# A two-layer graph transformer on one core: where lists, ranks, own queries, bias rows and the turned block stand in the order of the work

## The chip, the cores and the metric

The kernel runs on one core of a Trainium2 chip. The metric is the device time of one execution in microseconds (us); the time of a kernel is the median of its runs. A profiled execution gives a span (first to last instruction of the core), a trace of every instruction, and the clock granted to TensorE.

## What is computed

Two layers of the same graph transformer on 2,708 tokens of 512 numbers. The adjacency matrix is sparse (some ten neighbours for a token, itself among them). All numbers are float32.

```python
def layer(h, adj, ...):                      # 8 heads of 64, feed-forward of 2048
    mask = adj + eye(n)
    q, k, v = (h @ Wq.T + bq), (h @ Wk.T + bk), (h @ Wv.T + bv)
    scores = where(mask == 0, -1e9, q k^T / sqrt(64))      # per head
    attn_out = (softmax(scores) @ v) @ Wo.T + bo
    h1 = layer_norm(h + attn_out, ln1_g, ln1_b)
    ff = relu(h1 @ W1.T + b1) @ W2.T + b2
    return layer_norm(h1 + ff, ln2_g, ln2_b)
```

## The kernel before, in words

**Tiles and places.** `by_edges` (L480) does all the work (`by_rows` runs only if a flag says that the lists did not fit; here they do). Tokens are worked in 22 tiles of 128, the last with 20. The kernel finds each token's list of neighbours, ranks the tokens by the length of their lists, and from then on a tile is 128 places in that order, so that all tokens of tile g have at most `CAPS[g]` neighbours. Keys and values of a tile's neighbours are gathered from DRAM row by row (`gather`, L1076, an indirect DMA that GpSimd, POOL, issues), one slot of the list at a time.

**Stage 1, `first` (L874).** For each of the 22 tiles in their first order TensorE makes keys and values (`project`, L577: four matmuls of 128x512, each in two passes). ScalarE copies them out of PSUM, POOL adds bk to the keys, and ScalarE's DMA queue writes them to `kv_d`. Beside that, `lists` (L685) turns rows of the adjacency matrix, loaded by SyncE (SP), into lists on VectorE (DVE); `counted` (L722) counts and numbers them and leaves `hot`, `before` and the record `rec`. bk and bq come as columns (`given_column`, L558) and are turned into rows that all partitions hold (`turned_row`, L563: four 128x128 diagonals on VectorE, four matmuls by ones on TensorE, a copy).

**Stage 2, `first_queries` (L951).** 22 tiles of queries (`evicted`, L957, on VectorE; `written`, L964, stores two tiles at a time by SyncE). At t = 1 `ranked` (L783): four matmul pairs `pr` (L790, L797), a chain of VectorE steps, and the write of `rec` to `rec_d` in the first order of the tokens (L811, L815, on ScalarE's queue). At t = 4 `inverted` (L853) gives `ident_i`, the token at each place; the keys of tile 21 are finished (`last_keys`, L943); the lists of the first two tiles (`list_of`, L1017), the rows of x of the first three (`own_rows`, L1020, `xr`) and the first gathers of keys are issued on POOL. At t = 7 (`OWN`) the three `xr` are turned (`flip`, L1246: four transposes on TensorE, a copy on ScalarE) and two tiles' queries made of them; the third follows at t = 12. `LISTS` holds the t at which two more lists are gathered. `beside_queries` (L1625) loads W1 and W2 and advances the attention.

**Attention, `attend` (L1540).** A generator whose steps are chunks of two slots: VectorE multiplies keys by the query and sums (L1114, L1120); one step later ScalarE takes exponentials and scales values (`p`, L1133; L1140) and VectorE scales and adds the rest; later still the sums are divided (`cx`, L1184). `advance` (L1597) emits steps as credit allows:

```python
        credit = min(credit + more, 1.5)
        while credit > 0 and len(got) < CXB:
            cost = next(ahead, None)
            if cost is None:
                break
            credit -= cost
```

A step costs 1 for two slots. `None` comes back when a tile's query is not to be had: beyond the first three tiles of `order` (20, 19, 18; then 17) queries of layer 0 are fetched from `q_d` (`asked`, L1086), which needs all of them written.

**Feed-forward.** Blocks of two tiles. For each of 16 f: four matmuls `pf` (L1458), a Relu `ft` on ScalarE (L1469) and, LAG = 3 later, the second product `a` (L1431). `pf` has three PSUM buffers. In between stand the next block's output projection and norm (`attended`, L1379, through `cT`) and its transposition (`turned`, L1402: two flips into the one buffer `hT`), the keys and values of layer 1 (`keys_values`, L1498), and steps of attention by the paces `PACES` and `PACE`. `load_next` (L1315) fetches the biases that layer 1 needs.

**Layer 1's queries** are made of transposed tiles `zT_d` by `Layer.query` (L1349) and stored by `kept` (L1362); eight tiles are loaded ahead (`preloaded`, L1322), the others pass through `queries` (L1335) with three buffers.

The order on every engine is the program's order: all five are scheduled by hand, each engine works and waits in order, and so does each engine's DMA queue.

Of the kernel before, what the change touches and what calls it, by code (L numbers as in the profile page):

```python
# [18 lines left out]
P = 128  # L19
DM = 512  # L20
# [26 lines left out]
OWN = 7  # L47
LISTS = (6, 9, 11, 14, 15, 17, 18, 19, 20, 21)
# [431 lines left out]
def by_edges(ctx: ExitStack, tc: tile.TileContext, x, xT, adj, layers, out, redo):  # L480
# [34 lines left out]
    own = {}  # L515
    all_made = []
# [12 lines left out]
    ident_i = const.tile([P, NT], I32, name="ident_i")  # L529
    flags = const.tile([P, 4 + NL], F32, name="flags")  # L530
# [6 lines left out]
    rec_d = dram.tile([N, 2 * LIST], F32, name="rec_d")  # L537
# [20 lines left out]
    def given_column(w, name):  # L558
        t = small.tile([P, NC], F32, tag=name, name=name, bufs=1)
        nc.sync.dma_start(out=t, in_=w[name])  # L560
        return t

    def turned_row(col, name, scale):  # L563

        t = rows.tile([P, DM], F32, tag=name, name=name)
        dg = dn.tile([P, NC, P], F32, tag="row", name="dg", bufs=3)
        for c in range(NC):
            nc.vector.tensor_scalar(
                dg[:, c, :], ident, col[:, c : c + 1], scale, ALU.mult, ALU.mult
            )  # L570
        yield t
        pr = ps.tile([P, DM], F32, tag="g", name="pr")
        for c in range(NC):
            nc.tensor.matmul(pr[:, c * P : (c + 1) * P], ones, dg[:, c, :], start=True, stop=True)
        nc.vector.tensor_copy(t, pr)
# [39 lines left out]
    def lists_of(pa):  # L615
# [167 lines left out]
        def ranked(hot, before, half):  # L783

            at = pa.tile([P, NT], F32, tag="at", name="at", bufs=1)
            for h in range(2):
# [24 lines left out]
            nc.scalar.dma_start(  # L811
                out=rec_d[: (NT - 1) * P, :].rearrange("(g p) c -> p g c", p=P),
                in_=rec[:, : NT - 1, :],
            )
            nc.scalar.dma_start(out=rec_d[(NT - 1) * P :, :], in_=rec[:LW, NT - 1, :])  # L815
# [37 lines left out]
        def inverted(parts):  # L853
# [16 lines left out]
            nc.vector.tensor_tensor(ident_i, sums[:, :NT], sums[:, NT:], ALU.add)  # L870

        return lists, counted, (ranked, inverted)

    def first(w, meanwhile):  # L874
# [27 lines left out]
        for c in range(NC):  # L902
            nc.sync.dma_start(out=wk[:, c, :], in_=chunked(w["Wk"])[:, c, :])
            if c == 0:
                cols = [given_column(w, "bk")]
        cols.append(given_column(w, "bq"))
        finish(halves)
        turning = turned_row(cols[0], "bk", 1.0)
        bk = next(turning)
        turning_q = turned_row(cols[1], "bq", DK**-0.5)  # L910
        bq = next(turning_q)
        wv = matrix(w, "Wv", "wv")
        pa = tc.tile_pool(name="pa", bufs=2)
        lists, counted, placing = lists_of(pa.__enter__())
        done, before = 0, None
        for t in range(NT):
            r = size(t)
            xs = tokens(t, 0)
            kv = wts.tile([P, 2 * DM], F32, tag=f"w2_{5 + t % 3}", name="kvs")
            k = project(xs, r, wk, "k")  # L920
            if t == 0:
                finish(turning)
                finish(turning_q)
# [16 lines left out]
            if t == QT:  # L940
                wq = matrix(w, "Wq", "wq", nc.gpsimd)

# [6 lines left out]
        return bq, wq, counts, placing, pa, tokens, last_keys  # L949

    def first_queries(bq, wq, counts, placing, pa, tokens, last_keys, meanwhile):  # L951

        nonlocal at
        ranked, inverted = placing
# [19 lines left out]
        for t in range(NT):  # L974
# [4 lines left out]
            if t == 1:  # L979
                parts = ranked(*counts)  # L980
                evicted(0, held, qs)
            if t == 4:
# [7 lines left out]
                for g in order[:2]:  # L990
                    list_of(g)
                xrs = [own_rows(g) for g in order[:3]]
# [4 lines left out]
            if t == 0:  # L997
                held = q
            else:
                evicted(t, q, qs)  # L1000
# [4 lines left out]
            if t == OWN:  # L1005
                zTs = [turned_own(g, xr) for g, xr in zip(order, xrs)]
# [3 lines left out]
            if t == OWN + 5:  # L1010
                own_query(order[2], zTs[2], to[order[2]], bq, wq)
# [5 lines left out]
    def list_of(g):  # L1017
        gather(listed[: size(g), g, :], rec_d, ident_i[: size(g), g : g + 1])
# [801 lines left out]
```

## Time and profile before

| what | us |
|---|---|
| median of 3 runs (1875.48 to 1880.53) | 1876.91 |
| the profiled execution | 1872.77 |
| its span | 1871.0 |
| stage 1, to the last values of tile 21 | 0 to 154.7 |
| stage 2, to the last query matmul | 154.6 to 262.5 |
| layer 0's feed-forward begins | 264.6 |
| layer 1's queries begin with tile 3 of its order | 1103.4 |
| layer 1's feed-forward begins | 1179.7 |
| TensorE's last matmul ends | 1861.8 |

The mean granted clock is 0.996. The DMA engines are busy 80 to 100% of the time in the first 180 us (300 to 400 GB/s) and less later (195 GB/s over the span). Rows of a timeline give start, duration, engine, line, operation, tiles written and read, how many instructions are merged, and in brackets the engine's idle time before and what ended it. `PE` is a matmul, `ACT` ScalarE, a name with q a DMA queue.

### The profile page before, as it was taken

The numbers are of one execution on the slowest core, as the hardware profiler recorded it, in microseconds if no ns is written. First come the engines' busy times: TensorE is split into PE (matmuls) and PEld (weight loads), VectorE is DVE, ScalarE is ACT, GpSimd is POOL, SyncE is SP. The second block draws the span as 40 slices with busy tenths as digits, with TensorE's granted clock in tenths as the row PEclk, the third lists the DMA queues.
The fourth block names the chain that finished last, engine by engine and source line by source line (L and its number), as shares of the span: only waits on it lengthen the run. The fifth ranks groups of instructions, "written<-read, shape, count | busy, mean of one in ns | idle before, by whom it ended". The sixth has DMA issues, their size and how long they took to land.

```text
span 1871.0 us, 20950 instructions
## 1 busy us (share of the span) xinstructions
PE 1834.5 (98%) x6172; PEld 1090.1 (58%) x6172; DVE 1378.4 (74%) x2160; ACT 941.9 (50%) x3261; POOL 778.7 (42%) x743
## 2 busy tenths in 40 slices
PE   8999899999999999999999999999999999999997
PEld 4444455665656656566565544566666666566664
DVE  6886569876777868678674147878888988789842
ACT  5670336555445555555643213556655675557531
POOL 3233655443544435343531033444553655356302
PEclk9999899999999999999999999999999999999999
DMA  9999867646545455463541676836554664446300
GB/s 334 356 333 307 308 207 265 205 145 208 186 147 182 165 195 195 159 200 116 182 160 45 210 243 259 308 122 229 186 204 156 241 220 164 179 170 207 126 1 20
DMA packets 134411, 366.93 MB, mean 196 GB/s; under 512 B 19636, under 2 KB 37892, under 8 KB 134286
## 3 DMA queue, kind: packets, MB, share of 16 engines
q0 software_dynamic: 70608, 252.12, 39.5%
q1 hardware_dynamic: 50754, 90.23, 14.0%
q10 hardware_dynamic: 12924, 23.15, 3.3%
q8 instruction: 50, 0.82, 0.2%
q14 instruction: 75, 0.61, 0.1%
HBM read 314.79 MB, written 50.65 MB: 195 GB/s over the span
## 4 chain that ended last, share of the span: by engine, by line
PE 86%; DVE 5%; DMA 4%; ACT 2%; issue 2%; POOL 0%; SPq 0%; ACTq 0%; POOLq 0%; DVEq 0%
PE pf L1458 29%; PE a L1431 28%; PE k L587 8%; PE v L587 8%; PE o L587 7%; PE q L587 3%; PE tp L1250 2%; DVE kv L1114 1%; DMA rec_d<-rec 1%; DVE sc L1120 1%; ACT kv L1140 1%; DVE kv L1146 1%; DMA w<-in_W 1%; PE a L1446 1%; ACT cx L1184 1%
## 5 line engine op out<-in xcount | busy, mean ns | idle before, releaser
L1458 PE MATMUL pf<-hT,w 128*128 128x256 f32 (+1 forms) x2816 | 631.5, 371 | 8.0 <-ACT hT L1255 6.3
L1458 PEld LDWEIGHTS pf<-hT,w 128*128 128x128 f32 x2816 | 517.5, 190 | 180.9 <-issue 101.5
L1077 POOL DMA_INDIRECT kv<-kv_d,listed x420 | 504.3, 1201 | 281.0 <-issue 117.2
L1431 PE MATMUL a<-w,ft 128*128 128x512 f32 x1312 | 611.1, 592 | 0.0
L1469 ACT ACTIVATE ft<-pf,b 128x256 f32<-128x256 f32 (+1 forms) x336 | 154.9, 463 | 453.4 <-PE pf L1458 453.3
L1431 PEld LDWEIGHTS a<-w,ft 128*128 128x128 f32 x1312 | 246.8, 190 | 187.4 <-issue 170.9
L1240 POOL TENSOR_TENSOR rd<-va,mhalf 128x1 f32<-128x1 f32 (+1 forms) x88 | 81.6, 928 | 561.1 <-DVE va L1238 561.1
L1140 ACT ACTIVATE kv<-kv,p 128x64 f32<-128x64 f32 x1232 | 311.0, 334 | 5.0
L1114 DVE TENSOR_TENSOR kv<-kv,q 128x1024 f32<-128x1024 f32 (+1 forms) x222 | 256.7, 1157 | 12.7 <-DMA q<-q_d,ident_i 11.6
L1120 DVE TENSOR_REDUCE sc<-kv 128x16 f32<-128x1024 f32 (+1 forms) x222 | 257.9, 1162 | 7.6
L1153 DVE TENSOR_TENSOR acc<-acc,kv 128x1024 f32<-128x1024 f32 (+2 forms) x178 | 205.3, 1154 | 76.7 <-ACT kv L1140 65.8
L1133 ACT ACTIVATE p<-sc,listed 128x8 f32<-128x8 f32 x420 | 103.6, 295 | 132.5 <-DVE sc L1120 121.8
L1146 DVE TENSOR_TENSOR kv<-kv,p 128x512 f32<-128x512 f32 (+1 forms) x178 | 122.9, 690 | 44.0 <-ACT p L1133 44.0
L587 PE MATMUL o<-wo,cT 128*128 128x512 f32 x336 | 148.1, 593 | 1.0 <-ACT cT L1255 1.0
L587 PEld LDWEIGHTS o<-wo,cT 128*128 128x128 f32 x336 | 63.5, 190 | 81.9 <-issue 75.1
L1244 DVE SCALAR_TENSOR_TENSOR h<-h,rd,ln_b 128x512 f32<-128x512 f32 (+1 forms) x88 | 66.1, 751 | 39.9 <-POOL rd L1240 39.9
L1184 ACT ACTIVATE cx<-acc,su 128x64 f32<-128x64 f32 (+1 forms) x352 | 88.3, 333 | 12.9 <-DVE su L1176 7.7
L707 DVE MAX8 tops<-code 128x8 f32<-128x247 f32 (+2 forms) x242 | 78.6, 400 | 18.2 <-ACT code L702 18.2
L1140 ACT ACTIVATE acc<-kv,p 128x64 f32<-128x64 f32 (+1 forms) x352 | 88.8, 335 | 1.4
L1393 DVE TENSOR_TENSOR h<-o,xb 128x512 f32<-128x512 f32 (+1 forms) x44 | 30.2, 687 | 73.0 <-PE o L587 51.5
L587 PE MATMUL k<-wk,xg 128*128 128x512 f32 x168 | 77.1, 602 | 5.1 <-DMA wk<-in_Wk 5.1
L1518 ACT COPY kvs<-v 128x512 f32<-128x512 f32 (+1 forms) x22 | 12.9, 586 | 132.9 <-PE v L587 131.9
(170 smaller groups left out, 1596.2 us busy)
## 6 DMA issues: line engine op xcount, KB each, us to landing
aj<-in_adj SPq DMA_DIRECT2D x42, 677.0 KB, 6.6
kv_d<-kvs ACTq DMA_DIRECT2D x21, 512.0 KB, 6.9
xg<-in_xT SPq DMA_DIRECT2D x19, 512.0 KB, 6.5
w<-in_W SPq DMA_DIRECT2D x16, 512.0 KB, 5.9
kv<-kv_d,listed POOLq DMA_INDIRECT x420, 5.9
zT_d<-zT SPq DMA_DIRECT2D x22, 256.0 KB, 5.6
xb_d<-h SPq DMA_DIRECT2D x21, 256.0 KB, 5.8
q<-q_d SPq DMA_DIRECT2D x21, 256.0 KB, 4.1
```

The costliest lines, as they stand in the source:

```text
L587: nc.tensor.matmul(o[:r], xs(c), wm[:, c, :], start=(c == 0), stop=(c == NC - 1))
L1077: return nc.gpsimd.indirect_dma_start(out=to, out_offset=None, in_=table[:, :], in_offset=bass.IndirectOffsetOnAxis(ap=s, axis=0), bounds_ ...
L1114: nc.vector.tensor_tensor(kv[:r, :c, :DM], kv[:r, :c, :DM], self.q[:r].unsqueeze(1).to_broadcast([r, c, DM]), ALU.mult,)
L1120: nc.vector.tensor_reduce(self.sc[:r, s0 : s0 + c, :], kv[:r, :c, :DM].rearrange("p s (h d) -> p s h d", d=DK), AX.X, ALU.add,)
L1133: nc.scalar.activation(p[:r, s, :], self.sc[:r, s, :], AF.Exp, bias=minus[:r, g, s : s + 1])
L1140: nc.scalar.activation(to[:, i, hd], kv[:r, i, DM + h * DK : DM + (h + 1) * DK], AF.Copy, scale=p[:r, s0 + i, h : h + 1],)
L1146: nc.vector.tensor_tensor(to[:, 0, :].rearrange("p (h d) -> p h d", d=DK), kv[:r, 0, DM:].rearrange("p (h d) -> p h d", d=DK), p[:r, s0, : ...
L1153: nc.vector.tensor_tensor(self.acc[:r, :c, :], self.acc[:r, :c, :], kv[:r, :c, DM:], ALU.add)
L1184: nc.scalar.activation(cx[:r, hd], self.acc[:r, 0, hd], AF.Copy, scale=self.su[:r, h : h + 1])
L1431: nc.tensor.matmul(a[:r], fts[f][:, c0 : c0 + r], self.w2[f // 2][:, f % 2, :], start=(f == 0), stop=(f == NFC - 1),)
L1458: nc.tensor.matmul(pf[:, :w], self.w1[f // 2][:, c, f % 2 * P : f % 2 * P + P], hT[:, c, :w], start=(c == 0), stop=(c == NC - 1),)
L1469: nc.scalar.activation(ft[:, :w], pf[:, :w], AF.Relu, bias=self.b1[:, f : f + 1])
```

## The change

It has these parts:

- `rec_d` holds one row of 22 records for each lane (partition), and is written by one DMA ahead of the last tile's keys; `place_i` gives the row of a place's record.
- `ranked` stands ahead of the keys of tile 21 (the small tile); `inverted` and what follows stand at t = 2.
- OWN = 5 and earlier `LISTS`; the third tile is turned when its query is made.
- The columns bk and bq are written to a DRAM line by a DMA of single elements and loaded as a row; POOL scales bq. `turned_row` goes.
- W1 and W2 of the first four pairs of f are loaded at t = 8, 10, 12, 14 of stage 2 (before: at the end of stage 1 and t = 0, 1), the fifth at t = 16 (before 6).
- `hT` of the next block is copied ahead of the step of f = 15.
- Layer 1: two more transposed tiles are loaded into the `hT` buffer, queries are stored by SyncE, except for a middle stretch that ScalarE's queue stores.

```diff
-OWN = 7
-LISTS = (6, 9, 11, 14, 15, 17, 18, 19, 20, 21)
+OWN = 5
+LISTS = (4, 7, 9, 12, 13, 14, 15, 17, 18, 19)
...
-    rec_d = dram.tile([N, 2 * LIST], F32, name="rec_d")
+    rec_d = dram.tile([P * NT, 2 * LIST], F32, name="rec_d")
...
+    def lined(w, name, by):
+
+        line = dram.tile([1, DM], F32, name=f"{name}_d{len(lines)}")
+        lines.append(line)
+        by.dma_start(out=line.rearrange("o (c p) -> p (o c)", p=P), in_=w[name])
+        return line
+
+    def row_of(line, name, scale=None):
+
+        t = rows.tile([P, DM], F32, tag=name, name=name)
+        nc.sync.dma_start(out=t, in_=line.to_broadcast([P, DM]))
+        if scale is not None:
+            nc.gpsimd.tensor_scalar(t, t, scale, None, ALU.mult)
         return t
...
-            nc.scalar.dma_start(
-                out=rec_d[: (NT - 1) * P, :].rearrange("(g p) c -> p g c", p=P),
-                in_=rec[:, : NT - 1, :],
-            )
-            nc.scalar.dma_start(out=rec_d[(NT - 1) * P :, :], in_=rec[:LW, NT - 1, :])
+            nc.scalar.dma_start(out=rec_d.rearrange("(p t) c -> p t c", p=P), in_=rec)
...
             nc.vector.tensor_tensor(ident_i, sums[:, :NT], sums[:, NT:], ALU.add)
+            nc.vector.tensor_scalar(sums[:, :NT], sums[:, :NT], NT, None, ALU.mult)
+            nc.vector.tensor_scalar(sums[:, NT:], sums[:, NT:], 1.0 / P, None, ALU.mult)
+            nc.vector.tensor_tensor(place_i, sums[:, :NT], sums[:, NT:], ALU.add)
...
-            if c == 0:
-                cols = [given_column(w, "bk")]
-        cols.append(given_column(w, "bq"))
+        short = [lined(w, name, nc.scalar) for name in ("bk", "bq")]
...
         wv = matrix(w, "Wv", "wv")
+        bk = row_of(short[0], "bk")
...
             r = size(t)
+            if t == NT - 1:
+                parts = placing[0](*counts)
             xs = tokens(t, 0)
...
+            if t == NT - 4:
+                bq = row_of(short[1], "bq", DK**-0.5)
...
-            if t == 1:
-                parts = ranked(*counts)
-                evicted(0, held, qs)
-            if t == 4:
+            if t == 2:
                 inverted(parts)
...
-                for g in order[:2]:
-                    list_of(g)
-                xrs = [own_rows(g) for g in order[:3]]
+                list_of(order[0])
+                xrs = [own_rows(g) for g in order[:2]]
+                list_of(order[1])
+                xrs.append(own_rows(order[2]))
...
-                zTs = [turned_own(g, xr) for g, xr in zip(order, xrs)]
+                zTs = [turned_own(g, xr) for g, xr in zip(blocks[0], xrs)]
...
-                own_query(order[2], zTs[2], to[order[2]], bq, wq)
+                own_query(order[2], turned_own(order[2], xrs[2]), to[order[2]], bq, wq)
...
+            self.stores = nc.sync
...
-                by = nc.scalar if self.apart else nc.sync
-                by.dma_start(out=q_d[self.n][g * P : g * P + r, :], in_=qs[:r])
+                self.stores.dma_start(out=q_d[self.n][g * P : g * P + r, :], in_=qs[:r])
...
-            now.load_w1(t + 2 - NT, nc.gpsimd)
-            now.load_w2(t + 2 - NT, nc.gpsimd)
...
-        if t < 2:
-            now.load_w1(t + 2, nc.gpsimd)
-            now.load_w2(t + 2, nc.gpsimd)
+        if t in (8, 10, 12, 14):
+            now.load_w1(t // 2 - 4, nc.gpsimd)
+            now.load_w2(t // 2 - 4, nc.gpsimd)
         if t == 6:
             now.settle()
+        if t == 16:
             now.load_w1(4, nc.scalar)
             now.load_w2(4, nc.scalar)
...
-            streamed = now.queries(order[8:16])
+            streamed = now.queries(order[10:16])
...
+            both = dn.tile([P, 2, NC, P], F32, tag="hT", name="zTs", bufs=1)
+            for i, g in enumerate(order[8:10]):
+                nc.sync.dma_start(out=both[:, i], in_=zT_d[n][g])
+                pool.append((g, both[:, i]))
             next(streamed)
+            now.stores = nc.scalar
...
+                if i == 4:
+                    now.stores = nc.sync
...
+                if more and f == NFC - 1:
+                    finish(asking)
+                    hT = now.turned(blocks[k + 1], hs_next)
                 advance((PACE if k else PACES)[n][f])
                 if f in (0, 3, 7, 9):
                     next(asking, None)
-                if more and f == NFC - 1:
-                    finish(asking)
-                    hT = now.turned(blocks[k + 1], hs_next)
...
-                    if f == 0 and k in (1, 3):
-                        i, name, scale = (1, "bk", 1.0) if k == 1 else (0, "bq", DK**-0.5)
-                        turning = turned_row(now.cols[i], name, scale)
...
+                    if (k, f) == (1, 0):
+                        now.bk = row_of(now.short[0], "bk")
+                        nxt.bq = row_of(now.short[1], "bq", DK**-0.5)
```

## The prediction, made before the changed kernel was run

> **What bounds the kernel now.** I read the page's busy shares first, then who waited for whom on TensorE, then the timelines of all engines around each wait.
>
> ```profile
> PE 1834.5 (98%) x6172; PEld 1090.1 (58%) x6172; DVE 1378.4 (74%) x2160; ACT 941.9 (50%) x3261; POOL 778.7 (42%) x743
> ```
>
> TensorE is busy 98%, so the end moves only by TensorE work that is removed or TensorE waits that are. The 36.5 us of idle time are 5.07 at the start, some 9.4 behind the last matmul, and these:
>
> ```profile
> PE tp L1250 <- DMA xr<-in_x,ident_i: 7.9, 2, 6.5
> PE pf L1458 <- ACT hT L1255: 6.3, 4, 2.2
> ...
> PE q L587 <- DMA zT<-zT_d: 1.8, 2, 1.4
> PE k L582 <- ACT zT L1255: 1.3, 1, 1.3
> PE q L587 <- DVE qs L959: 1.0, 1, 1.0
> ```
>
> (columns: total us, times, longest). The largest, 7.9, goes back to the write of the lists; POOL and PE rows of the timeline (start, us, then the idle time before and its releaser):
>
> ```profile
> 183.39 1.12 POOL L1077 DMA_INDIRECT listed<-rec_d,ident_i  x1 [25.66 <-DMA rec_d<-rec]
> ...
> 192.83 0.45 PE L1250 MATMUL tp<-ident,xr 128*128 128x128 f32 x1 [6.55 <-DMA xr<-in_x,ident_i]
> ```
>
> The rec_d write took 27.2 us to land. In 2-us windows the granted clock falls behind that idle time:
>
> ```profile
> 186.00:188.00 2.00, 0.28 (x1) 0.00 (x0) 1.77 (x3) 0.00 (x0) 1.54 (x2) 1.00 1.03 394
> ...
> 190.00:192.00 2.00, 0.00 (x0) 0.00 (x0) 0.00 (x0) 0.00 (x0) 1.39 (x3) 0.50 1.00 342
> ...
> 196.00:198.00 2.00, 2.00 (x8) 1.48 (x7) 0.00 (x0) 1.17 (x2) 1.63 (x2) 0.50 1.03 416
> ...
> 200.00:202.00 2.00, 2.00 (x6) 0.82 (x5) 0.22 (x1) 0.00 (x0) 1.58 (x2) 1.00 1.04 404
> ```
>
> (the column behind the engines is the clock, then DMA share and GB/s). Last, the one place where attention holds up the feed-forward of layer 0: tile 17's query can be fetched only when all queries are written.
>
> ```profile
> 274.59 1.01 POOL L1077 DMA_INDIRECT q<-q_d,ident_i  x1 [0.95 <-DMA bq<-in_bq]
> ...
> 280.61 1.22 DVE L1114 TENSOR_TENSOR kv<-kv,q 128x1024 f32<-128x1024 f32 x1 [11.64 <-DMA q<-q_d,ident_i]
> ...
> 283.12 0.30 ACT L1133 ACTIVATE p<-sc,listed 128x8 f32<-128x8 f32 x1 [7.29 <-DVE sc L1120]
> ...
> 285.57 0.45 ACT L1469 ACTIVATE ft<-pf,b 128x256 f32<-128x256 f32 x1
> ...
> 291.70 0.48 PE L1458 MATMUL pf<-hT,w 128*128 128x256 f32 x1 [0.95 <-ACT ft L1469]
> ```
>
> ScalarE works in order: the Relu (ft) of f = 5 stood behind tile 17's first weights until 285.57. Three PSUM buffers and LAG = 3 let it cost TensorE only 0.95.
>
> **A. Bias rows through DRAM.** Four turned rows go: 16 matmuls of 128 columns, two passes each; the first eight took 1.78 in the chain, so 1.8 at the start and 1.8 in layer 0's feed-forward. VectorE loses their diagonal and copy steps, off the path. SyncE sheds two issues at 0.43, so Wk's chunks 2 to 4 come 0.5 sooner; tile 0's keys took 5.22 for 3.43 of work. That is worth up to 1.0; nothing before shows 4-byte writes to DRAM beside the first loads, which could cost as much. I take 0.3 (range -1 to +1). New waits: SyncE waits for the bk line, with two token loads and all adjacency loads behind. The nearest row is the 4-byte column bv, 8.5 us to landing on a busy DMA; the low end is the first loads' 4.9. DMA: Bandwidth & Descriptors, "Rules for kernel authors", says that a non-contiguous last dim becomes one descriptor per element and is to be avoided: 512 per line, against this change. The page gives no time for it, so the row prices it: issued at 0.9, landed at 5.8 (SyncE is there at 7.02 less two issues, 6.1: no wait) or at 9.4 (adjacency 2.6 late). Either costs TensorE nothing: VectorE's list steps have some 18 us of gaps between 20 and 143.  POOL gets two 128x512 scalings, 1.27 each by its bias addition: one in stage 1, ahead of a bias addition and Wo's loads, whose users come later; one in block 1, its row landed long before. Sum: -3.9.
>
> **B. Rank products first.** The four matmul pairs move, not shrink. `before` and `hot` are done at 150.66; TensorE would come at 152.77 - 2.1 = 150.7. No wait, or 0.5 if VectorE does not follow. VectorE's ranking (8.0, 162.67 to 170.7) then ends near 161, so the 1.0 wait on query evictions goes. -1.0.
>
> **C. Lists as one row a lane; own queries at 5.** 2,708 runs of 192 B become 128 of 4,224 B. Near row: kv_d, 512 KB, 6.9 to landing; far one: 27.2 as before. Issued near 153 it lands near 160, or at 180. I take 160: the eight W1/W2 loads (4 MB) that filled the DMA beside it move to tiles 8 to 14. ScalarE's second issue, stuck 19.4, goes. place_i (three VectorE steps at 0.18) is ready near 166, POOL's list and two row gathers issue by 170 at 1.3 apart, and xr lands by 175 (median gather 4.8; 7.3 when saturated); TensorE reaches the flips at 175.3. Cover gone: about 1. So -7.9, and the clock: the flips and queries behind ran 0.57 + 0.9 + 1.18 = 2.65 long. New: with two flips, then a lone third one, TensorE waits for ScalarE's copies, 0.3 and 0.9 (o waited 0.96 for cT): +1.2. POOL's eight W issues (0.75 each) now stand between gathers, but all eleven slots of tiles 20 and 19 are issued ahead of them, so block 0's attention doesn't wait; its two extra tiles are slack. w1_4/w2_4 on ScalarE's queue are needed 100 us later: nothing. Sum: -9.3.
>
> **D. What the earlier attention leaves.** Steps are emitted by credit, capped at 1.5. Attention now stops at tile 17's missing query three tiles before the end, so credit fills to 1.5 (0.5 before), and at f = 0 two steps come out instead of one. ScalarE's built order before: Relu 0, one p, Relus 1 to 4, then tile 17's p and eight scalings. After: Relu 0, three p, those eight scalings, then Relu 1. So Relu 1 waits for the fetched query. With T the end of the last query matmul (262.5 before): the last 20-row eviction, free of the attention step ahead of it, ends at T + 3.0 (before T + 6.5). From there to the blocked Relu's end took 17.06 (268.96 to 286.02), so T + 20.1, or T + 18.5 if the fetch takes the median 5.3 and the write less. pf starts at T + 2.1; four pf and one second product (5 x 1.72) bring TensorE to pf 4 at T + 10.7, which needs Relu 1's buffer. Idle: 7.8 to 9.4; I take 8.6. Then the clock. TensorE: Matmul & The Clock Gate, Part 1, says half rate after one idle window of about 3.4 us and full after 3.4 us of sustained work: 1.7 lost. The row shows half rate for 6.5 us behind the restart, a 1.33 gap in it, 2.65 lost. I take 2.2. Gone in exchange: 0.95, and 0.5 at the flips of block 1. Sum: +9.3.
>
> **E. hT ahead of the step.** Only the waits at 1441.80 (1.54) and 1634.67 (1.48) are of this kind; the other two hT waits stand before a loop. The copies need 2.2 and have 5.15 of second products as cover once no attention stands ahead. Attention's ScalarE part is 2.2 later, within VectorE's gaps (about 12% of a block there). -3.0 (range -3 to 0).
>
> **F. Layer 1's queries.** The stores move to SyncE: zT of the 20-row tile no longer waits behind two stores, -1.3; hT no longer behind the last one, -0.6. Behind the stores SyncE holds zT and q loads, which are early. Two more zT in the free hT buffer let the first critical load be issued when the rush of gathers ends (POOL's last at 1133): -1.3 of the 1.8. Sum: -3.2. Settling and list gathers at other tiles: nothing, VectorE and POOL have gaps there.
>
> **Sum.** -3.9 - 1.0 - 9.3 + 9.3 - 3.0 - 3.2 = -11.1. The profiled execution took 1872.77 (span 1871.0), so 1861.7; against the median of the runs, 1876.91, which lies 4.1 above it, 1865.8.
>
> **Rivals.** 1: the Relu block of D is small, since the query lands sooner or ScalarE isn't parked there. For it: VectorE is free at T; against: the fetch follows the last query, whatever came before. Without D: 20.4 less, 1856.5. 2: gathers starve. W loads among POOL's gathers and a DMA near 400 GB/s delay xr by 1 and the flips of block 0 by 4: 1871. For it: 213 to 389 GB/s already at 200 to 260; against: the order of the gathers. 3, slower: the write of the lists stays slow, for its cost lay in the loaded DMA (Wo and 0.5 MB of keys are still beside it), not in its short runs. Landing at L, it lets list and rows arrive at L + 8.5 (1.3, 1.0, and 6 to landing), and TensorE, which now comes two tiles sooner, at 175.3: from L = 167 on it waits. At 27.2 us again, L = 180.4, it waits 13.6 and the clock's 2.65 stays, so C is +6.9 and the sum +5.1: 1882; the sum turns at L near 175, 22 us to landing. Against: 512 KB of keys with runs of 4 KB landed in 6.9 on a DMA as busy.
>
> **Chances.** Forecast 0.64; rival 1 0.14; rival 2 0.12; rival 3 0.10. A measurement of this kernel can tell 0.3%, 5.6 us, from no change: faster is below 1871.3. Forecast and rival 1 are faster but for 0.05 of the forecast; rival 2 half and half; rival 3 is slower by over 0.3% in about half, with late starts of other kinds in the rest. Faster 0.79, same 0.14, slower 0.07. The range takes the forecast's own (1861 to 1871) and most of rivals 1 and 2: 1855 to 1873.
>
> **What would show it.** Right: no xr wait and full clock near 175; a TensorE gap of some 8 us at f = 4 of block 0, released by ft, with the clock at 0.5 behind it; no 128x128 `pr`; rec_d landing below 10 us; no hT waits beyond 1400. Wrong: a wait at `pr` of the ranks or at tile 0's keys (bias lines), xr waits, new waits of tp for cx.

## The result, and the profile after

The changed kernel takes 1880.69 us (median; 1877.88 to 1882.99), the kernel before 1874.62 (1872.73 to 1880.53): a ratio of 1.0029, 95% interval 1.0022 to 1.0036. It is slower by about 5.5 us, where 11 less were forecast, and lies outside the range of 1855 to 1873. The profiled execution's span is 1879.0 (1871.0 before). These are the busy shares of the changed kernel, and its waits on TensorE (columns: total us, times, longest):

```profile
PE 1833.0 (98%) x6140; PEld 1087.8 (58%) x6140; DVE 1373.1 (73%) x2143; ACT 944.1 (50%) x3261; POOL 781.8 (42%) x745
```

```profile
PE pf L1445 <- ACT ft L1456: 15.6, 1, 15.6
PE k L585 <- DMA wk<-in_Wk: 11.6, 1, 11.6
PE tp L1237 <- DVE qs L951: 2.2, 1, 2.2
PE pf L1445 <- ACT hT L1242: 1.5, 2, 1.1
PE tp L1237 <- ACT cx L1171: 1.2, 2, 1.0
```

The xr waits (7.9), those for zT_d (1.8) and the two of hT behind 1400 are gone, as forecast. In their place stand one forecast wait at twice its size (ft, 15.6) and one that was not forecast at all: Wk, 11.6 where the kernel before has

```profile
PE k L587 <- DMA wk<-in_Wk: 5.1, 1, 5.1
```

Where each kernel is, at the same six points of the work:

| point (start of the instruction) | before | after | difference | step of it | forecast |
|---|---|---|---|---|---|
| last small tile; before its keys, after its ranks | 152.77 | 158.43 | +5.7 | +5.7 | -2.1 (A) |
| end of the last query (T) | 262.5 | 257.3 | -5.2 | -10.9 | -10.3 (B, C) |
| sixth first product of block 0 | 276.81 | 293.57 | +16.8 | +22.0 | +10.8 (D) |
| flips of h ahead of layer 1's small tile | 1092.11 | 1105.09 | +13.0 | -3.8 | -3.3 (A, D) |
| first product of layer 1 | 1179.65 | 1190.19 | +10.5 | -2.4 | -3.2 (F) |
| end of the span | 1871.0 | 1879.0 | +8.0 | -2.5 | -3.0 (E) |

(The forecast's D is split here: 8.6 and 2.2 at the stall; 0.95 and 0.5 given back later, with 1.8 of A.) Four of the six agree within 1. The other two, 7.8 and 11.2 off, are nearly the whole miss, which is 19.1 in the spans.

**The start.** ScalarE's queue issued the two lines at 0.81 and 1.49, SyncE's queue Wk's four chunks from 1.31 to 3.35. The timeline of TensorE in the changed kernel, then the waits of SyncE's queue (SPq):

```profile
11.57 5.50 PE L585 MATMUL k<-wk,xg 128*128 128x512 f32 x8 [11.57 <-DMA wk<-in_Wk]
```

```profile
SPq L552 <- DMA bk_d<-in_bk: 7.5, 1, 7.5
...
SPq L552 <- DMA bq_d<-in_bq: 2.4, 1, 2.4
```

Wk was issued as early as before, and still its keys began 6.5 later; Wv (L552) was issued at 11.30, 6.6 later than before. In 2-us windows (the last three columns are the granted clock, the DMA share and GB/s) the bytes stop while the DMA engines stay busy (first the changed kernel, then the one before):

```profile
4.00:6.00 2.00, 0.00 (x0) 0.00 (x0) 0.00 (x0) 0.00 (x0) 2.00 (x2) 1.00 1.56 156
6.00:8.00 2.00, 0.00 (x0) 0.00 (x0) 0.00 (x0) 0.00 (x0) 2.00 (x4) 1.00 1.09 27
```

```profile
4.00:6.00 2.00, 0.93 (x1) 0.50 (x2) 0.77 (x2) 0.00 (x0) 2.00 (x2) 1.00 0.98 326
6.00:8.00 2.00, 2.00 (x4) 0.76 (x3) 2.00 (x3) 0.00 (x0) 2.00 (x2) 1.00 1.00 245
```

The DMA queues of the first 12 us (packets, MB, share of 16 engines), after and then before:

```profile
q1 hardware_dynamic: 1066, 1.21, 76.9%
q10 hardware_dynamic: 1056, 0.00, 9.2%
```

```profile
q1 hardware_dynamic: 2997, 3.13, 83.7%
```

q10 holds the elements of the two lines. They themselves take 9%, but each packet of the loads (q1) now takes 0.769 x 16 x 12 / 1066 = 138 ns, before 54 (packets of some 1.1 KB in both). The bytes are also fewer because SyncE issued nothing more between 3.8 and 11.3: Wv is late a second time over, for a reason that lies in the program. In the built program each transfer issued by an engine's own queue reports to one of eight semaphores in turn, and the one that takes a semaphore next waits until the one before has landed:

```
L552 DMACopy wv<-in_Wv 128x512 [waits DMAHW0_49]
...
L552 DMACopy wv<-in_Wv 128x512 [waits DMAHW2_49]
```

DMAHW0 is the semaphore of bk_d, DMAHW2 that of bq_d: Wv's first and third chunk waited 7.5 and 2.4 for the two lines, and no data connects them. Wk's four chunks and the first tokens are among the first eight transfers and wait for no semaphore; what is late there is their landing.

**The lists.** POOL and TensorE of the changed kernel:

```profile
174.62 1.13 POOL L1064 DMA_INDIRECT listed<-rec_d,place_i  x1 [17.41 <-DVE place_i L867]
```

```profile
183.69 1.04 PE L1237 MATMUL tp<-ident,xr 128*128 128x128 f32 x8
```

The write of the lists was issued at 160.5 and landed 7.0 later. The list gather waits for place_i, no longer for the write; the flips come without a wait, and the granted clock is 1.00 in the windows from 182 to 188.

**The stall.** VectorE, SyncE's queue, POOL, ScalarE and TensorE of the changed kernel, in order of time, and last SyncE's row of the kernel before (VectorE's step between the fetch and `p` began at 282.90):

```profile
250.70 0.69 DVE L1380 TENSOR_TENSOR h<-o,xb 128x512 f32<-128x512 f32 x1 [10.00 <-DMA xb<-in_x,ident_i]
```

```profile
264.53 3.05 SPq L964 DMA_DIRECT2D q_d<-qs  x2
267.63 0.68 SPq L564 DMA_DIRECT2D bk_d<-in_bk  x1
```

```profile
278.43 1.00 POOL L1064 DMA_INDIRECT q<-q_d,ident_i  x1 [11.49 <-DMA bo<-in_bo]
```

```profile
285.42 0.49 ACT L1120 ACTIVATE p<-sc,listed 128x8 f32<-128x8 f32 x2 [19.93 <-DVE sc L1107]
...
287.87 1.17 ACT L1456 ACTIVATE ft<-pf,b 128x256 f32<-128x256 f32 x3
```

```profile
288.38 3.63 PE L1445 MATMUL pf<-hT,w 128*128 128x256 f32 x8 [15.63 <-ACT ft L1456]
```

```profile
262.99 6.31 SPq L972 DMA_DIRECT2D q_d<-qs  x2
```

This is the chain of D, link by link, but two links are later than forecast. VectorE met rows (xb) that were 10 us late, so the last eviction ended at T + 10.0, not T + 3.0. And layer 1's lines, which SyncE issues right behind the last query's store because it runs ahead, are in front of the fetch: 10.85 from the end of the last store's issue to the fetch (267.58 to 278.43), 5.3 before (269.30 to 274.59). Between 272 and 278 the DMA moved nothing.

How they delay it can be read from the landings. In the built program the fetch waits for the stores of the queries alone (the trace names bo, which only landed last). A landing is told by sixteen signals on the transfer's semaphore. Of the store issued at 264.53, ahead of the lines, fifteen came by 270.00 and the last at 277.48; the fetch began 0.95 after it. In the kernel before the last signal of a store came at 273.73, 0.86 ahead of the fetch. So the lines need not land before the fetch: they hold a part of a store that was issued before them.

### The profile page after: what moved, and what is told of

The parts are those of the page before. It is cut to its first block, busy times and chain, and to the rows that moved or that the text cites. A ratio compares the mean times of both kernels' runs of the same rounds, so it can differ in the third digit from the quotient of the medians.

```text
span 1879.0 us, 20852 instructions
## 1 busy us (share of the span) xinstructions
PE 1833.0 (98%) x6140; PEld 1087.8 (58%) x6140; DVE 1373.1 (73%) x2143; ACT 944.1 (50%) x3261; POOL 781.8 (42%) x745
## 3 DMA queue, kind: packets, MB, share of 16 engines
q1 hardware_dynamic: 53106, 93.63, 14.5%
## 4 chain that ended last, share of the span: by engine, by line
PE 88%; DVE 4%; DMA 4%; issue 2%; ACT 1%; POOL 1%; ACTq 0%; POOLq 0%; SPq 0%; DVEq 0%
PE pf L1445 29%; PE a L1418 29%; PE v L585 8%; PE k L585 8%; PE o L585 7%; PE q L585 4%; PE tp L1237 2%; DVE kv L1101 1%; DMA kv<-kv_d,listed 1%; DVE sc L1107 1%; DMA bq_d<-in_bq 1%; DMA q_d<-qs 1%; ACT kv L1127 1%; PE a L1433 1%; DMA xb<-in_x,ident_i 0%
## 5 line engine op out<-in xcount | busy, mean ns | idle before, releaser
L1445 PE MATMUL pf<-hT,w 128*128 128x256 f32 (+1 forms) x2816 | 634.7, 373 | 18.7 <-ACT ft L1456 15.6
L585 PE MATMUL k<-wk,xg 128*128 128x512 f32 x168 | 77.4, 604 | 11.6 <-DMA wk<-in_Wk 11.6
L700 ACT ACTIVATE code<-aj 128x1354 bf16<-128x1354 int32 (+1 forms) x44 | 72.8, 1720 | 19.0 <-POOL aj L694 13.8
```

The costliest lines, as they stand in the source:

```text
L585: nc.tensor.matmul(o[:r], xs(c), wm[:, c, :], start=(c == 0), stop=(c == NC - 1))
L1445: nc.tensor.matmul(pf[:, :w], self.w1[f // 2][:, c, f % 2 * P : f % 2 * P + P], hT[:, c, :w], start=(c == 0), stop=(c == NC - 1),)
```

## The experiments

Theory: the single-element writes (A) cost the start and, in layer 0, lengthen a stall (D) that the attention's credit causes; everything else does what was forecast. Rivals: the two stalls have one cause; the fetch is late because VectorE is; the write of the lists is fast only for the emptier DMA beside it. All ratios are to the kernel before, measured on the same chip, with 95% intervals. Experiments 1 to 4 ran on one chip, 5, 6, 8 and 9 on a second, 7 and 10 to 12 on a third, so two experiments of different chips are compared with more doubt; spans of the profiled executions stand beside the ratios where the two differ.

### 1. Bias rows as before

```diff
-        short = [lined(w, name, nc.scalar) for name in ("bk", "bq")]
+                cols = [given_column(w, "bk")]
...
-            self.short = [lined(nxt, name, nc.sync) for name in ("bk", "bq")]
+            self.cols = given_column(nxt, "bq"), given_column(nxt, "bk")
```

(and the rest of A undone: `turned_row` in both layers.)

> The changed kernel with its bias rows turned on TensorE as before, in both layers (no line through DRAM); everything else as changed. Theory (the single-element writes clog the DMA at the start, and once more hold up tile 17's query in layer 0): the key product of the last small tile comes 5.7 us sooner (152.8), the fetch of tile 17's query no longer waits 11.5 us, so the stall of TensorE for ft falls from 15.6 to about 10; four turned rows cost 1.8 in the feed-forward again. Together about -9.5 against the changed kernel: 1871, ratio to before 0.998. Rival (the lines cost the start alone; the fetch is late because the last query is): -4, stall still 15 or more, ratio 1.001.

Measured: 1870.9, ratio 0.9981 (0.9973 to 0.9988). The first keys start at 4.64, and in TensorE's and POOL's rows the fetch and the stall are shorter:

```profile
278.85 3.42 PE L1470 MATMUL pf<-hT,w 128*128 128x256 f32 x8 [9.17 <-ACT ft L1481]
```

```profile
269.95 1.00 POOL L1089 DMA_INDIRECT q<-q_d,ident_i  x1 [6.09 <-DMA bo<-in_bo]
```

So both costs of A are real: the start, and 6.5 of the 15.6. What is left of the stall, 9.2, is there without any line.

### 2. Credit 0.5 at the start of the feed-forward

```diff
+        if n == 0:
+            credit = min(credit, 0.5)
         for k, block in enumerate(blocks):
```

> The changed kernel with the attention's credit held to 0.5 when layer 0's feed-forward begins, so that one step and not two comes out at f = 0, and ScalarE's order there is that of before. Theory (Relu 1 is parked behind tile 17's query only by that order): the stall of 15.6 at the fifth first product goes, and the clock stays at 1.00; Relu 5 then stands behind that query and costs about 3 at the ninth. About -14.5: 1866, ratio 0.9955. Rival (the stall comes from the late last query eviction, whatever the order): the stall stays above 8, ratio above 0.999.

Measured: 1869.55, ratio 0.9970 (0.9961 to 0.9980): 11 less than the changed kernel, not 14.5. The clock stays at 1.00 from 266 to 294, but three waits of 0.91, 1.99 and 1.91 remain at pf (expected: one of 3), and ScalarE's rows show a reason:

```profile
280.84 0.41 ACTq L1273 DMA_DIRECT2D w<-in_W  x1
281.30 0.84 ACT L1456 ACTIVATE ft<-pf,b 128x256 f32<-128x256 f32 x2 [10.20 <-DMA bk_d<-in_bk]
```

The Relus stand in ScalarE's order behind the issue of a W2 load, and that issue waits for bk_d's landing: the turn of semaphores again (in the built program its semaphore is that of layer 1's bk_d). The rival, that the late eviction alone makes the stall, falls.

### 3. Both

> Both edits: bias rows turned as before, credit 0.5. Theory: the start is that of before, no stall above 2 at the start of block 0's feed-forward, everything else as changed. About -21 against the changed kernel: 1860, ratio 0.992. Rival (the two stalls share one cause, so the second edit adds nothing to the first): within 4 of the better of the two single edits, 1866.

Measured: 1861.0, ratio 0.9926 (0.9908 to 0.9944). Both costs go, and they add. So the change without its bias lines and with one number in the credit is 0.7% faster than the kernel before. What is left of trouble there is shorter: TensorE waits 2.44 at the flips for an eviction, then

```profile
257.04 9.53 PE L1470 MATMUL pf<-hT,w 128*128 128x256 f32 x32 [0.46 <-ACT hT L1267]
```

The 32 matmuls took 7.17 in the kernel before; here the clock had fallen during the first of the two waits:

```profile
258.00:260.00 2.00, 2.00 (x6) 1.58 (x5) 2.00 (x4) 0.00 (x0) 1.39 (x3) 0.50 0.47 85
```

It was 0.75 from 254 to 256, 0.50 from 256 to 260 and 0.54 from 260 to 262. In all 2.44 + 0.46 + 2.36 = 5.3, where 1.05 (the hT wait of before) would be. The clock's part is not the same in every execution: experiment 8 has the same wait at the flips (2.59), and its clock did not fall.

### 4. Bias lines alone, on the kernel before

```diff
-                cols = [given_column(w, "bk")]
+        short = [lined(w, name, nc.scalar) for name in ("bk", "bq")]
```

(and the rest of A, as in the change.)

> The kernel before with only the bias rows taken through DRAM, in both layers. Theory: first key product near 11.6 (5.1 before), +5.7 by the last small tile; -1.8 in the feed-forward of layer 0; the fetch of tile 17's query 5.7 later, which the wait for ft at the ninth first product (0.95 before) shows as 6 to 7. About +9.5: 1884, ratio 1.005. Forecast's own value for this part: -3.9, ratio 0.998. Rival (start only): +4, ratio 1.002.

Measured: 1879.54, ratio 1.0028 (1.0020 to 1.0036): slower, but by 5.2, not 9.5. Wk costs 11.4 as in the full change. Two more waits of TensorE (a third, 2.7 for tokens at 177.7, the kernel before does not have, and the one for zT_d is 3.1 instead of 1.8):

```profile
PE pf L1449 <- ACT ft L1460: 3.6, 2, 3.3
PE tp L1241 <- DMA xr<-in_x,ident_i: 3.4, 1, 3.4
```

Two sizes were off. With everything later, the write of the lists had more time, so xr waits 3.4 instead of 7.9; and ft waits 3.6, not 6 to 7. The direction is clear: A by itself, forecast at -3.9, costs about 5.

### 5. Residual rows two tiles sooner

```diff
+        if t == 12:
+            early_xbs.extend(now.residuals(blocks[0]))
         if t == NT - 6:
             through(0)
-            early[0] = now.attended(blocks[0], got)
+            early[0] = now.attended(blocks[0], got, early_xbs)
```

> Bias rows turned as before, credit 0.5, and the two row gathers for block 0's residual put on GpSimd's queue two tiles sooner (at tile 12 of the queries), ahead of the gathers of four lists and five key-value slots. Theory (VectorE came 10 us late to the end of the queries because those rows were queued behind other gathers): VectorE's wait for xb (10.2 in that kernel) and TensorE's wait of the flips for an eviction (2.4) go; -2.4: 1858.5, ratio 0.9913. Rival (the DMA is full, so the key-value gathers that now come later take the wait over): same time within 1, 1861.

Measured: 1855.2, ratio 0.9908 (0.9894 to 0.9922). The flips no longer wait for an eviction, VectorE's first addition of xb waits only for its product (1.98), and the clock is 1.00 in all windows from 248 to 260. By the ratios that is 3.4 less than experiment 3, with intervals that overlap; by the spans 4.9, which agrees with the 5.3 - 1.05 = 4.2 counted there. The expectation of 2.4 had left out the clock, whose part is chance (experiment 3).

### 6. W1 and W2 loads at their old places

> Bias rows turned as before, credit 0.5, and the ten W1/W2 loads of the query stage at the tiles of the kernel before (four pairs around the last keys, the fifth at query tile 6), where they fill the DMA beside the write of the lists. Theory (the one-row-a-lane write is fast of itself, since its runs are long): it lands within 10 us of its issue (27.2 before), TensorE waits for xr by less than 1; and the later gathers meet an emptier DMA, so the late residual rows (2.4 on TensorE) are on time: 1858.5, ratio 0.9913. Rival (the write was slow for the load beside it): 20 us to landing, xr waits of 5 or more and half clock, 1868 or more, ratio 0.9965.

Measured: 1860.22, ratio 0.9934 (0.9921 to 0.9946). This tells apart why the write of the lists became fast. The DMA issues between 150 and 185 of this kernel (KB each, us to landing):

```profile
w<-in_W POOLq DMA_DIRECT2D x8, 512.0 KB, 15.9
...
rec_d<-rec ACTq DMA_DIRECT2D x1, 528.0 KB, 11.6
```

With 4 MB of weights beside it the one-row-a-lane write lands in 11.6 (expected: under 10), the old one took 27.2; xr costs TensorE 0.40. So the new layout (long runs, one issue instead of two) did most of it, and rival 3 of the prediction falls. The rows came in time, as expected, but the time did not fall, since the product behind the third flip now waited 3.67 for ScalarE's copy, behind a step of attention, and the clock was at 0.50 from 207.7 to 211.1.

### 7. One line instead of two at the start

```diff
-        short = [lined(w, name, nc.scalar) for name in ("bk", "bq")]
+        short = [lined(w, name, nc.scalar) for name in ("bk",)]
+        cols = [given_column(w, "bq")]
```

> Bias rows as before and credit 0.5 (the third kernel of the first call), but bk of layer 0 through DRAM, written by ScalarE ahead of Wk's chunks as in the changed kernel; bq turned. Half the dose of single-element writes. Theory (the DMA engines are held for a time in proportion to the 4-byte elements): first keys near 7.9 instead of 4.6 (11.6 with both lines), 0.9 of turned row saved: +2.5, 1863, ratio 0.994. Rival (any such write at the head costs the whole delay, since SyncE's wait for the line is what holds Wv and the tokens): first keys near 11, +5.5, 1866.5, ratio 0.9955.

Measured: 1865.88, ratio 0.9970 (0.9959 to 0.9981), on the base of experiment 3: 0.9926. That is 8 by the ratios (two chips) and 5.0 by the spans.

```profile
9.90 5.38 PE L604 MATMUL k<-wk,xg 128*128 128x512 f32 x8 [9.90 <-DMA wk<-in_Wk]
```

```profile
6.00:8.00 2.00, 0.00 (x0) 0.00 (x0) 0.00 (x0) 0.00 (x0) 2.00 (x4) 1.00 0.53 26
```

The dose is not proportional: one line costs the first keys 5.3 (4.64 to 9.90), the second 1.7 more. The rival's number is nearer than the theory's, but not its reason: SyncE's wait cannot hold Wk, which had been issued by 3.2. The landings show where the time goes. Taken in order of time, the sixteen signals of the line come from 7.10 to 9.60 and those of Wk's first chunk from 7.27 to 9.77, each 0.15 to 0.20 behind the line's. In the changed kernel the pairs run from 6.68 and 6.86 to 11.28 and 11.44, 0.16 to 0.21 apart; with turned rows the chunk has landed at 4.51. So Wk's first chunk lands when the line does: the first line costs its own landing, and the second makes the first 1.7 longer. Why a line of 2 KB takes that long is not shown.

### 8. Layer 1's lines later

```diff
-            self.short = [lined(nxt, name, nc.sync) for name in ("bk", "bq")]
+            self.short = [lined(nxt, name, nc.scalar) for name in ("bk", "bq")]
...
-                    if (k, f) == (0, 9):
+                    if (k, f) == (0, 11):
                         now.load_next()
```

> Bias rows of layer 0 turned as before, credit 0.5; those of layer 1 through DRAM, but issued by ScalarE at f = 11 of block 0, behind the fetch of tile 17's query, instead of by SyncE, which ran ahead. Theory (only what is queued beside or behind the single-element writes pays): the two turned rows of layer 1 are saved, 1.8: 1859.2, ratio 0.9916. Rival (the writes cost as much wherever they are put): the gathers of block 1 or layer 1's Wk and Wv come 6 to 10 us late, TensorE waits at block 1: 1863 or more.

Measured: 1859.0, ratio 0.9930 (0.9917 to 0.9943); experiment 3 has 0.9926. The lines land 11.6 and 12.7 after their issue at 300.8 and 301.4. Three gathers of keys issued beside them (300.5 to 303.7) land 11.7, 12.9 and 14.5 after their issue, the same three in experiment 5, without lines, 7.5, 8.7 and 9.4; so the neighbours are held here too, but nobody on TensorE waits in block 1. The rival's time falls, its mechanism does not; whether the 1.8 is gained, the interval can't tell.

### 9. Layer 0's lines behind the first loads

```diff
         wv = matrix(w, "Wv", "wv")
+        short = [lined(w, name, nc.sync) for name in ("bk", "bq")]
```

> Credit 0.5, layer 1's rows turned; layer 0's rows through DRAM, but the two writes issued by SyncE behind Wk, the first tokens and Wv (ScalarE ahead of them in the changed kernel), bk's row fetched by GpSimd. Theory (the cost at the start is the place in front of Wk): first keys near 4.6 as with turned rows, their 1.8 saved: 1859.2, ratio 0.9916; adjacency later by some 6, which VectorE's gaps take. Rival (the writes stop the DMA for 6 us wherever they are): TensorE waits for tokens, Wv or a buffer of keys between tile 0 and 5, by 3 or more: 1864 or more, ratio 0.9945.

Measured: 1864.38, ratio 0.9952 (0.9940 to 0.9964): the rival. TensorE's row, and the window in which the bytes stop:

```profile
17.28 2.08 PE L604 MATMUL v<-wv,xg 128*128 128x512 f32 x2 [4.34 <-DMA wv<-in_Wv]
```

```profile
12.00:14.00 2.00, 0.94 (x3) 0.12 (x1) 0.00 (x0) 0.00 (x0) 0.00 (x0) 1.00 0.71 20
```

Wv's four issues were over at 5.9 and bk_d's began at 6.52, and still TensorE waits 4.3 for Wv's last chunk: loads already issued are held as well. It was issued at 5.46; six of its sixteen signals came by 10.61, the others, among those of the lines, until 17.24. No turn of semaphores is in this. The clock adds to it, which the theory and the rival had both left out:

```profile
18.00:20.00 2.00, 2.00 (x3) 0.67 (x2) 0.00 (x0) 0.59 (x1) 1.76 (x2) 0.50 0.56 87
```

It was at 0.50 from 15.4 to 22.2.

### 10 and 11. hT behind the step, and layer 1's opening as before

```diff
-                if more and f == NFC - 1:
-                    finish(asking)
-                    hT = now.turned(blocks[k + 1], hs_next)
                 advance((PACE if k else PACES)[n][f])
...
+                if more and f == NFC - 1:
+                    finish(asking)
+                    hT = now.turned(blocks[k + 1], hs_next)
```

> The fastest kernel so far (bias rows as before, credit 0.5, residual rows two tiles sooner) with hT copied behind the attention step again. Forecast's step E: the hT waits at two blocks of layer 1 come back, +3.0: 1858.2, ratio 0.9924. Rival (the wait moves to another buffer, so the order is worth nothing): 1855.2, ratio 0.9908.

```diff
-                self.stores.dma_start(out=q_d[self.n][g * P : g * P + r, :], in_=qs[:r])
+                by = nc.scalar if self.apart else nc.sync
+                by.dma_start(out=q_d[self.n][g * P : g * P + r, :], in_=qs[:r])
...
-            streamed = now.queries(order[10:16])
+            streamed = now.queries(order[8:16])
```

(and the rest of F undone.)

> The same fastest kernel with layer 1's opening as before (stores on ScalarE, two zT fewer ahead, attention steps at the old places). Forecast's step F: the zT wait of 1.3 at the 20-row tile, 1.3 of zT loads and 0.6 at hT come back, +3.2: 1858.4, ratio 0.9925. Rival (the waits are replaced by the new ones for cx, 1.2): +2 or less, 1857, ratio 0.9917.

Measured: 1858.2, ratio 0.9930 (0.9916 to 0.9943), and 1857.2, ratio 0.9928 (0.9915 to 0.9942), against 1855.2 and 0.9908 for experiment 5; by the spans 2.2 and 1.0 more. All three intervals overlap, so the waits must tell. With hT behind, those of 1.53 and 1.47 at 1427 and 1620 are back: step E's 3.0, and its rival falls. With layer 1's opening undone, these are back:

```profile
PE pf L1470 <- ACT hT L1267: 3.5, 2, 2.4
...
PE k L599 <- ACT zT L1267: 1.3, 1, 1.3
```

With 1.6 for zT_d and 0.7 for cT, and 1.4 more at hT than in experiment 5, that is 5.0 of waits more, and 1.65 of the new ones for cx less: 3.3. But the sixteen matmuls behind the new waits for cx tell of another cost, the clock. Experiment 5, then 11:

```profile
1141.36 8.58 PE L604 MATMUL o<-wo,cT 128*128 128x512 f32 x16
```

```profile
1142.08 7.13 PE L604 MATMUL o<-wo,cT 128*128 128x512 f32 x16 [0.68 <-ACT cT L1267]
```

In experiment 5 it was at 0.50 from 1140.9 to 1144.3, in 11 not. From the first of these queries to the first product of the feed-forward both take the same, 76.1 and 76.0. So step F's waits go as forecast, but little more than the 1.3 at the small tile is left of the 3.2: the rival's time, 1857, is the one measured, though the ratio is nearer to the forecast's.

### 12. Put together

```diff
+            if t == OWN + 4:
+                lone = turned_own(order[2], xrs[2])
             if t == OWN + 5:
-                own_query(order[2], turned_own(order[2], xrs[2]), to[order[2]], bq, wq)
+                own_query(order[2], lone, to[order[2]], bq, wq)
```

(with the edits of 2, 5, 8 and layer 0's rows turned.)

> Put together: layer 0's bias rows turned, layer 1's through DRAM by ScalarE at f = 11 of block 0; credit 0.5; residual rows two tiles sooner; and the lone third flip one query tile ahead of its product, so that TensorE doesn't wait for ScalarE's copy (1.4 in all kernels with the new lists). Theory: -1.8 and -1.4 against 1855.2: 1852, ratio 0.989. Rival (the flip finds its rows or ScalarE late a tile earlier, the lines cost what they save): 1855, ratio 0.9908.

Measured: 1851.69, ratio 0.9898 (0.9883 to 0.9914): faster than both kernels, and 1.0% faster than the one before. Its interval overlaps experiment 5's. The sum of the theory came out, but not by its two terms alone: the clock is at full speed from 8.4 to 1844.8, which saves what experiment 5 loses at 1141, and a wait of 1.1 is new. The lone flip costs nothing now; the largest wait on TensorE behind Wk (4.5) and hT (2.1) is

```profile
PE pf L1472 <- DVE qs L616: 1.1, 1, 1.1
```

## Why the prediction was wrong, point by point

**A failed, and with it the sign.** The step was "issued at 0.9, landed at 5.8 ... or at 9.4 ... Either costs TensorE nothing". It priced the line's own landing, and asked who waits for the line. It did not ask what the line does to the loads beside it. One line lands in 8.8 when alone (experiment 7), close to the upper end taken, and in 10.5 beside the second; but Wk's first chunk lands with it, so that Wk is held by 5.3 and, with two lines, by 6.9. "Wk's chunks 2 to 4 come 0.5 sooner" was no bound for that. The rule weighed there, of the Trainium skill's DMA: Bandwidth & Descriptors ("Rules for kernel authors"), had the right sign; the row taken in its place, bv, gave the landing of the small transfer and was not applied to its neighbours. In the change A costs about 9 (1.0029 to 0.9981, experiment 1; 5.2 alone, experiment 4), against -3.9: 12.9 of the 16.5 by which the forecast missed.

**A's second cost was left out.** Of layer 1's lines the forecast says only that the row of bk is "landed long before" its scaling. SyncE issues them ahead of their place in the program, just behind the last query's store, which POOL's fetch waits for and which they hold. For POOL and ScalarE the forecast asked what a moved step stands in front of; for SyncE at this place it did not.

**B and C were right.** 10.9 gained between the last small tile and T, 10.3 forecast. No xr wait, clock 1.00, and behind the flips idle times of 0.24 (which the trace does not put down to zT) and 0.85 where 0.3 and 0.9 were put. Experiment 6 shows that the new layout did most of it, with 11.6 to landing under the load that had made it 27.2.

**D was right in mechanism and size, for the kernel it was worked out for.** Without the lines the stall is 9.17 (7.8 to 9.4 forecast), and the credit is worth 10.3 (0.9981 to 0.9926, experiments 1 and 3; 9.3 forecast). The step inside it that failed is "the last 20-row eviction ... ends at T + 3.0": it ended at T + 10.0, and in experiment 1 at T + 11.0, for the late xb rows. TensorE came to the blocked product late as well (T + 16.5 in experiment 1, T + 10.7 forecast), so the difference held: that the size is so near is in part luck. In the changed kernel the lines added 6.5 to the stall. Of the clock's price two values were weighed, 2.65 by the row of before and 1.7, an estimate from a figure of the Trainium skill (TensorE: Matmul & The Clock Gate, Part 1), and 2.2 taken. The row here has 3.63 for eight matmuls that take 1.89, so 1.7: the estimate by the page was the better one.

**Rival 2 was half true.** xr was not late, but the rows for block 0's residual were, behind the W loads on POOL and in the DMA (382 GB/s on average between 205 and 250, 265 in the kernel before): 2.2 at the flips, 0.46 at hT, 0.8 at pf, and the clock, by which the first sixteen matmuls of pf took 5.29 instead of 3.7. Experiment 5 takes them away. So the mechanism of the rival was there beside the forecast's, at another gather than the one that it named.

**E was right, F in its waits:** 2.5 and 2.4 in the profile, 3.0 and 3.2 forecast. E's 3.0 is what the waits of experiment 10 show. F's new waits for cx (1.2; "new waits of tp for cx" stood among the signs of being wrong) and the clock behind them (0.50 from 1165.6 to 1169.0 in the changed kernel) had no term in its sum; in experiment 11 they take most of what F gives.

**The sum by the ratios.** A +9.0, D about +10.3, the rest -13.9 (experiment 3): +5.4, which is the result, 1.0029. That it adds up is no proof, since each term is the difference of two of these ratios; experiments 2 and 3 give A 8.2 and D 11.1 in the other order. The forecast had -3.9, +9.3 and -16.5.

## What to carry to other kernels

Price a DMA of many tiny elements by what it does to the transfers beside it, also those issued before it, which here landed with it: put it where no load is on the critical path, or keep 2 us of TensorE work instead. Of each new transfer ask at what time its queue really issues it (a queue without waits runs far ahead of the program's place), and which later issue takes the same completion semaphore. When work is made earlier, look at what stops it then: a credit that fills up releases more steps at once than before, on an engine that works in order.

## What was not expected of the hardware

- With two writes of 512 single floats, 4 KB in all, the loads of the first 12 us came to 101 GB/s instead of 261; each packet of the loads took 138 ns instead of 54. Transfers issued before them are held too (experiment 9), and for a store of queries in the changed kernel it was one signal of sixteen that came 7.5 behind the others.
- The first such line costs the first keys 5.3, the second 1.7 more: Wk's first chunk lands some 0.2 behind the line (experiment 7).
- The granted clock fell late in the long stall and early in a short wait. Idle from 272.75, it was still 1.00 from 276 to 278:

```profile
278.00:280.00 2.00, 0.00 (x0) 0.00 (x0) 0.00 (x0) 0.00 (x0) 1.27 (x2) 0.52 0.21 79
290.00:292.00 2.00, 2.00 (x7) 1.61 (x6) 1.93 (x5) 0.00 (x0) 1.23 (x3) 0.57 0.97 317
```

  In experiment 3, idle from 253.03, it fell at 255.0, and in experiment 8 a wait as long left it at 1.00. It came back 3.4 us after the long stall's end and 4.8 after the short one's (261.8). Between start and end of these kernels every stretch at 0.50 in their traces lasted 3.41 us or a whole multiple of it (3.41, 6.83, 10.24, 13.65), which fits a clock that is set anew at fixed intervals of 3.41, wherever a wait lies in them.
